# Experts' results written over their gathered rows, without clearings, finished in groups of four

## The chip, the core and the metric

The kernel runs on one core of a Trainium2 chip. A core has five engines with queues of their own that work in order: TensorE (PE, its weight loads listed as PEld), VectorE (DVE), ScalarE (ACT), GpSimd (POOL) and SyncE (SP). They wait for each other by semaphores, and transfers run beside them. The metric is the device time of one execution in microseconds (us), the median of several runs.

## What is computed

A batch of 4 sequences of 1024 tokens of 256 numbers passes two layers, each with a residual: causal attention of 16 heads, and then a block with a second, small attention over the 4 sequences and a mixture of 8 experts. Only the experts' end matters here:

```python
h = _layernorm(x + attn_out, ln1_g, ln1_b)
flat = h.reshape(-1, C)
...
_, top_i = jax.lax.top_k(probs, 2)
assign = jnp.max(top_i, axis=-1)
...
for e in range(E):
    he = jax.nn.gelu(flat @ w1[e].T + b1[e], approximate=False)
    oe = he @ w2[e].T + b2[e]
    out = jnp.where((assign == e)[:, None], oe, out)
moe_out = out.reshape(T, B, C)
return _layernorm(h + moe_out, ln2_g, ln2_b)
```

Each token has one expert. Its row `h` goes through that expert, `h` is added, the sum is normalised, scaled by `ln2_g`, and the shift `ln2_b` and the residual are added.

## The kernel before

Most of the program is attention, and a scheduler written in Python lays out every engine's instructions by hand while the program is built. The change touches only the last stage, the tiles of the experts. Tokens are sorted by expert into 38 tiles of 128 rows. A first lot of 18 tiles (named 0_0 to 0_17) can be listed when six of the eight blocks of tokens are routed; the second lot of 20 (1_0 to 1_19) is listed after the last block (`tabulate_rest`, at about 745 us). A tile lives in a row buffer `given` of 128 x 512 numbers: the left half is `h`, the right half the residual plus `ln2_b`. There are 18 such buffers, used in turn, so tile 1_j takes the one of 0_j, and 1_18 and 1_19 those of 1_0 and 1_1.

Work on the tiles goes in steps (`tile_step`). A step calls `fetch`, which gathers one tile by an indirect DMA on POOL (L1813), then `finish` and then the stages A, B and C of three tiles, which I name so: A turns the rows (`mtp`, copied to `mt` by ScalarE), B is the hidden product (`hid`) and its Gelu (`ge`), C is the output product (`oe`). Two tiles' `oe` share one PSUM bank; in the second lot these are 1_1 with 1_2, 1_3 with 1_4 and so on. In most tiles of the second lot `h` is added on VectorE, in place over the left half of `given`; in the first lot and in the last two tiles PE adds it in PSUM (`by_product`).

Counting steps from the start, tile 1_j is gathered in step 23+j, has A in step 28+j, B in 29+j and C in 30+j. `finish` first takes each pair that is being finished one stage further, and then takes the next two tiles that are done. The stages of a pair of the second lot, tiles k and k+1 with k even, are:

- step 32+k: the adds, the statistics (`stats_v`, `mv_v`), `rstd` + eps on VectorE, and the root, a power of -1/2, on POOL (`norm_root`, L814);
- step 33+k: nothing, while tiles are waiting;
- step 34+k: on VectorE two operations per tile, (v - mean) x gain into a tile `o` (a ring of four buffers), and `o` x `rstd` + right half of `given`;
- step 35+k: for each tile on POOL a clearing of an unused tile (`spare`, L1928) and a scatter of `o` to the output, an indirect DMA (L1929).

When no tile is waiting any more (`experts.waiting()` is 0) the later stages run together: in step 48 the pair 14/15 has its results and its scatters, and 16/17 its root; 1_18 and 1_19 are finished singly, in steps 49 to 51. After step 32 VectorE also checks the softmax sums (`check_sums`), and after step 35 PE and VectorE form `odd`, which decides at the end whether a slower general program has to run.

Of the kernel before, what the change touches and what calls it, by code (L numbers as in the profile page):

```python
# [29 lines left out]
F32 = mybir.dt.float32  # L30
# [3 lines left out]
ALU = mybir.AluOpType  # L34
# [3 lines left out]
P = 128  # L38
B, T, C = 4, 1024, 256
# [46 lines left out]
B_IN, B_OUT, G1, B1, G2, B2, RB = 0, 3 * C, 4 * C, 5 * C, 6 * C, 7 * C, 8 * C  # L86
# [519 lines left out]
def fast_layer(ctx: ExitStack, tc: tile.TileContext, odd, x, wq, wk, wv, wp, w_in, w_out, w_r,  # L606
# [26 lines left out]
    nc = Core(tc.nc, told)  # L633
# [14 lines left out]
    def const(name, shape, dtype=F32, into=keep):  # L648
        return into.tile(shape, dtype, tag=name, name=name)
# [73 lines left out]
    def row(at, n=C):  # L723
        return row_sb[:, at - G1:at - G1 + n]
# [66 lines left out]
    def norm_tiles(name, tag=""):  # L791
        return [
            small.tile([P, B] + shape, F32, tag=kind + tag, name=f"{kind}_{name}")
            for kind, shape in (("stats", [6]), ("mv", [2]), ("rstd", []))
        ]

    def norm_one(tiles, i, src):
        stats, mv, _ = tiles
        nc.vector.bn_stats(stats[:, i], src)
        nc.vector.bn_aggr(mv[:, i], stats[:, i])  # L800

    def norm_end(tiles, n):
        _, mv, rstd = tiles
        nc.vector.tensor_scalar(rstd[:, :n], mv[:, :n, 1], EPS, None, ALU.add)
        return mv, rstd

    def norm_stats(src, n, name, tag=""):
        tiles = norm_tiles(name, tag)
        for i in range(n):
            norm_one(tiles, i, src(i))  # L810
        return norm_end(tiles, n)

    def norm_root(rstd, n):
        nc.gpsimd.tensor_tensor(  # L814
            rstd[:, :n], rstd[:, :n], minus_half.to_broadcast([P, n]), ALU.pow
        )
# [344 lines left out]
    class Routing:  # L1161
# [3 lines left out]
        def __init__(self):  # L1165
            self.placed = 0
# [270 lines left out]
    class Table:  # L1437
        pass

    spare = const("spare", [P, 1])  # L1440
    part = Routing()
    tables = []
    tiles_to_do = []
# [357 lines left out]
    late = {}  # L1801
# [97 lines left out]
                nc.tensor.matmul(self.v, ident, self.hx[:, :C], start=False, stop=False)  # L1899
            nc.tensor.matmul(self.v, sel, b_bf[1], start=False, stop=True)  # L1900

    def finish_tiles(two):

        n, name = len(two), two[0].name
        for t in two:
            if not t.by_product:
                own = t.hx[:, :C]
                nc.vector.tensor_tensor(own, own, t.v, ALU.add)
                t.v = own
        mv, rstd = norm_stats(lambda k: two[k].v, n, f"v_{name}", "_v")  # L1910
        norm_root(rstd, n)
        yield
        if experts.waiting():
            yield
        os = []
        for k, t in enumerate(two):
            o = late["work"].tile([P, C], F32, tag="o", name=f"o_{t.name}", bufs=4)
            nc.vector.scalar_tensor_tensor(
                o, t.v, mv[:, k, 0:1], row(G2), ALU.subtract, ALU.mult
            )  # L1920
            nc.vector.scalar_tensor_tensor(
                o, o, rstd[:, k:k + 1], t.hx[:, C:2 * C], ALU.mult, ALU.add
            )
            os.append(o)
        if experts.waiting():
            yield
        for t, o in zip(two, os):
            nc.gpsimd.memset(spare, 0.0)  # L1928
            ins = nc.gpsimd.indirect_dma_start(  # L1929
                out=out.rearrange("t n c -> (t n) c"),  # L1930
                out_offset=bass.IndirectOffsetOnAxis(ap=t.table.out_rows[:, t.j:t.j + 1], axis=0),
                in_=o, in_offset=None, bounds_check=B * T - 1, oob_is_err=False,
            )
            if late["n_out"]:
                tc.declare_no_dep(ins.ins, group="rows", reason="a token is in one tile")
            tc.add_to_no_dep_group("rows", ins.ins)
            late["n_out"] += 1

    class Experts:
# [3 lines left out]
        def __init__(self):  # L1943
            self.step, self.fetched = 0, []
            self.n_fetched = self.n_finished = 0
            self.under_way, self.done, self.finishing = [], [], []

        def fetch(self):
            self.step += 1
# [9 lines left out]
        def finish(self):  # L1959
            for it in list(self.finishing):  # L1960
                n, stages = it
                if next(stages, self) is self:
                    self.finishing.remove(it)
                    self.n_finished += n
            n = 1 if self.done and len(self.done) + len(self.under_way) + self.waiting() < 3 else 2
            if len(self.done) >= n:
                two, self.done = self.done[:n], self.done[n:]
                self.finishing.append((len(two), finish_tiles(two)))
                next(self.finishing[-1][1])

        def waiting(self):
            return len(tiles_to_do) + len(self.fetched)

        def left(self):
            return (len(tiles_to_do) + len(self.fetched)
                    + len(self.under_way) + len(self.done) + len(self.finishing))

        def advance(self, finish=True):
            if finish:
# [18 lines left out]
    experts = Experts()  # L1998


    class Running:
# [4 lines left out]
        def next(self):  # L2006
            self.kind = next(self.stages, "end")
            if self.kind != "end":
                self.kind, self.cost, *self.more = self.kind
# [261 lines left out]
    work = ctx.enter_context(pool("work", 2))  # L2271
# [76 lines left out]
    def tile_step(finish=True):  # L2348
        at = tile_begin()
        for on, cost in TILE:  # L2350
            if on != "DVE" or experts.finishing or len(experts.done) == 2:
                free[on] = max(free[on], at) + cost
        experts.fetch()
        experts.advance(finish)
# [21 lines left out]
    n = 0  # L2376
# [11 lines left out]
@with_exitstack  # L2388
def tile_layer(ctx: ExitStack, tc: tile.TileContext, *args):
    nc = tc.nc  # L2390
    flag = ctx.enter_context(tc.tile_pool(name="flag", bufs=1))
    odd = flag.tile([P, 1], I32, tag="odd", name="odd")
    fast_layer(tc, odd, *args)
    again = nc.values_load(
        odd[0:1, 0:1], min_val=0, max_val=1,
        skip_runtime_bounds_check_because="a comparison's result",
    )
    with tc.If(again > 0):
        general_layer(tc, *args)
# [75 lines left out]
```

## Time and profile before

| | us |
|---|---|
| median of 3 runs (836.48 to 842.09) | 839.2 |
| the profiled run | 839.28 |
| its span, from the first to the last instruction | 837.1 |
| last gather starts | 805.38 |
| last stage C on PE ends | 821.44 |
| last scatter starts | 828.95 |

The mean granted TensorE clock of the profiled run is 0.94. Busy over the span are PE 719.4 us (86%), DVE 544.6 (65%), ACT 416.6 (50%) and POOL 251.1 (30%). In tenths of each of 40 slices of the span (some 21 us each) POOL and PE read so:

```profile
PE   4988879995999999998989999999983689678982
...
POOL 5534102211113221102211212122130235637885
```

POOL works little in the middle of the program and most in the last five slices, which are the stage that the change touches. A timeline line reads: start, duration, engine, source line, operation, out<-in, count, and in brackets the idle time of the engine just before it with what ended that idle time. All instructions that pass through the wrapper of line 587 carry that line's number, so groups are told apart by their tiles.

### The profile page before, as it was taken

How to read it: one execution, taken by the hardware profiler on the slowest of the kernel's cores; microseconds unless marked ns; L12 is line 12 of the kernel's file. 1: busy time of each engine (PE TensorE's matmuls, PEld its weight loads, DVE VectorE, ACT ScalarE, POOL GpSimd, SP SyncE). 2: the span in 40 equal slices, each digit the busy share in tenths (PEclk: the TensorE clock that was granted, in tenths of full speed). 3: DMA queues.
4: the chain of work that ended last, by engine and by line, in shares of the span. 5: the costliest groups of instructions: out<-in, count | busy, mean ns of one | idle time of the engine just before them, and what ended most of it. 6: DMA issues, size and time to landing. Idle time of an engine off the chain costs nothing. (4 is left out here: it accounts for less than half of the span.)

```text
span 837.1 us, 22503 instructions
## 1 busy us (share of the span) xinstructions
PE 719.4 (86%) x8917; PEld 540.2 (65%) x8917; DVE 544.6 (65%) x1316; ACT 416.6 (50%) x625; POOL 251.1 (30%) x360
## 2 busy tenths in 40 slices
PE   4988879995999999998989999999983689678982
PEld 2766657674666756665667767787762368567772
DVE  7337224546678877946964739487695869884663
ACT  1455436563647556735654658578460235323540
POOL 5534102211113221102211212122130235637885
PEclk9799889998999999998999999999997699978997
DMA  7454444424344324333354635445315512333430
GB/s 215 117 148 137 143 134 134 144 63 123 94 119 129 108 77 147 98 104 95 93 142 141 185 109 144 123 126 158 94 53 195 177 37 90 93 97 120 124 103 24
DMA packets 75219, 99.56 MB, mean 119 GB/s; under 512 B 19496, under 2 KB 58723, under 8 KB 74596
## 3 DMA queue, kind: packets, MB, share of 16 engines
q1 hardware_dynamic: 64576, 79.63, 32.1%
q0 software_dynamic: 4864, 14.16, 5.6%
q10 hardware_dynamic: 5668, 4.25, 1.7%
q8 instruction: 73, 1.20, 0.6%
q14 instruction: 38, 0.31, 0.1%
HBM read 61.55 MB, written 35.12 MB: 115 GB/s over the span
## 5 line engine op out<-in xcount | busy, mean ns | idle before, releaser
L587 ACT ACTIVATE p<-sk 128x1024 f32<-128x1024 f32 (+1 forms) x320 | 287.0, 939 | 162.8 <-PE sk L587 147.8
L986 POOL TENSOR_SCALAR_AFFINE_SELECT p<-p 128x512 f32<-128x512 f32 (+1 forms) x160 | 103.6, 651 | 397.8 <-ACT p L587 395.9
L587 PE MATMUL sk<-slots 32*128 32x128 f32 (+1 forms) x3456 | 181.7, 328 | 21.2 <-DVE kq L587 10.0
L587 PEld LDWEIGHTS sk<-slots 32*128 32x128 f32 x3456 | 138.1, 188 | 64.9 <-issue 26.8
L587 PE MATMUL pv<-p,v 128*32 128x128 f32 (+1 forms) x3456 | 144.5, 314 | 10.4 <-ACT p L587 4.6
L587 PEld LDWEIGHTS pv<-p,v 128*32 128x32 f32 x3456 | 96.7, 111 | 48.3 <-issue 8.3
L587 PE MATMUL qkvp<-w_in,ut 128*128 128x264 f32 (+1 forms) x224 | 79.1, 489 | 0.0
L587 PEld LDWEIGHTS qkvp<-w_in,ut 128*128 128x128 f32 x224 | 40.3, 194 | 26.7 <-issue 22.4
L587 PE MATMUL oe<-w,ge 128*128 (+1 forms) x152 | 45.2, 423 | 12.9 <-DVE given L587 4.5
L587 PE MATMUL qkp<-xt,wqk 128*128 128x256 f32 x208 | 54.4, 407 | 0.2 <-ACT p L587 0.2
L1813 POOL DMA_INDIRECT given<-rows,rows x38 | 43.2, 1137 | 27.6 <-DVE at_t L587 11.6
L587 PE MATMUL hid<-mt,w 128*128 128x128 f32 x304 | 47.0, 293 | 0.5 <-ACT ge L587 0.5
L587 PEld LDWEIGHTS qkp<-xt,wqk 128*128 128x128 f32 x208 | 39.6, 200 | 11.1 <-issue 3.3
L587 ACT COPY qkv<-qkvp 128x512 f32<-128x512 f32 (+1 forms) x28 | 15.3, 555 | 58.5 <-PE qkvp L587 43.9
L587 PEld LDWEIGHTS hid<-mt,w 128*128 128x128 f32 x304 | 41.9, 200 | 2.0 <-ACT ge L587 1.0
L587 DVE COPY qkv<-qkvp 128x264 f32<-128x264 f32 x28 | 11.9, 431 | 46.9 <-PE qkvp L587 46.8
L1929 POOL DMA_INDIRECT out_dram<-o,out_rows x38 | 38.9, 1024 | 8.8 <-issue 6.3
L587 DVE TENSOR_REDUCE sc<-pr 128x64 f32<-128x1024 f32 x32 | 39.0, 1220 | 1.1
L587 PEld LDWEIGHTS oe<-w,ge 128*128 128x128 f32 x152 | 28.0, 205 | 17.8 <-DVE given L587 5.7
L587 DVE TENSOR_TENSOR pv<-qkv,sc 128x1024 f32<-128x1024 f32 x32 | 39.2, 1224 | 0.4 <-issue 0.3
L587 DVE TENSOR_TENSOR pr<-qkv 128x1024 f32<-128x1024 f32 x32 | 39.2, 1226 | 0.0
L587 PE MATMUL vp<-wv,xt 128*128 128x256 f32 x128 | 35.3, 423 | 0.0
(333 smaller groups left out, 1040.2 us busy)
## 6 DMA issues: line engine op xcount, KB each, us to landing
slots<-k SPq DMA_DIRECT2D x128, 80.0 KB
k<-kq SPq DMA_DIRECT2D x32, 256.0 KB
v<-v SPq DMA_DIRECT2D x16, 288.0 KB
v<-v SPq DMA_DIRECT2D x4, 1152.0 KB
x<-in_x_dram SPq DMA_DIRECT2D x16, 256.0 KB
y<-yt SPq DMA_DIRECT2D x16, 256.0 KB
rows<-x SPq DMA_DIRECT2D x32, 128.0 KB
slots<-k SPq DMA_DIRECT2D x64, 64.0 KB
```

The lines of the kernel that those rows point to most:

```text
L587: ins = made(*args, **kwargs)
L986: nc.gpsimd.affine_select(blocks, blocks, pattern=[[0, 2], [0, size], [1, P]], compare_op=ALU.is_ge, fill=0.0, base=0, channel_multiplier=-1,)
L1813: nc.gpsimd.indirect_dma_start(out=self.hx, out_offset=None, in_=t.rows_of, in_offset=bass.IndirectOffsetOnAxis(ap=t.rows_[:, self.j:self. ...
L1929: ins = nc.gpsimd.indirect_dma_start(out=out.rearrange("t n c -> (t n) c"), out_offset=bass.IndirectOffsetOnAxis(ap=t.table.out_rows[:, t. ...
```

## The change

Results go over the left half of `given`, where the rows `h` were, instead of into a tile `o`. The clearing before each scatter is gone. Taking a pair is split into `measure_tiles` (adds and statistics) and `finish_tiles` (root, results, scatters), and a group of tiles is finished when it holds tiles added by PE, or four tiles, or when fewer than four tiles are still on their way. The first lot and tiles 1_18 and 1_19 stay in the groups they had. In a group of four the results and the scatters are given out two tiles per step while tiles are waiting.

```diff
-    spare = const("spare", [P, 1])
...
-    def finish_tiles(two):
+    def measure_tiles(tiles, two):
+        if not tiles:
+            tiles.extend([norm_tiles(f"v_{two[0].name}", "_v"), []])
+        norms, group = tiles
         for t in two:
             if not t.by_product:
                 own = t.hx[:, :C]
                 nc.vector.tensor_tensor(own, own, t.v, ALU.add)
                 t.v = own
-        mv, rstd = norm_stats(lambda k: two[k].v, n, f"v_{name}", "_v")
+        for t in two:
+            norm_one(norms, len(group), t.v)
+            group.append(t)
+
+    def finish_tiles(norms, group):
+        n = len(group)
+        mv, rstd = norm_end(norms, n)
         norm_root(rstd, n)
         yield
         if experts.waiting():
             yield
-        os = []
-        for k, t in enumerate(two):
-            o = late["work"].tile([P, C], F32, tag="o", name=f"o_{t.name}", bufs=4)
...
+        for lo in range(0, n, 2):
+            if lo and experts.waiting():
+                yield
+            for k, t in list(enumerate(group))[lo:lo + 2]:
+                o = t.hx[:, :C]
...
         if experts.waiting():
             yield
-        for t, o in zip(two, os):
-            nc.gpsimd.memset(spare, 0.0)
+        for k, t in enumerate(group):
+            if k == 2 and experts.waiting():
+                yield
+            o = t.hx[:, :C]
             ins = nc.gpsimd.indirect_dma_start(
...
-                self.finishing.append((len(two), finish_tiles(two)))
-                next(self.finishing[-1][1])
+                measure_tiles(self.measured, two)
+                in_psum = any(t.by_product for t in self.measured[1])
+                if in_psum or len(self.measured[1]) > 2 or self.open() < 4:
+                    norms, group = self.measured
+                    self.measured = []
+                    self.finishing.append((len(group), finish_tiles(norms, group)))
+                    next(self.finishing[-1][1])
+
+        def open(self):
+            return self.waiting() + len(self.under_way) + len(self.done)
```

A row buffer is counted as free for the next gather when the finishing of its whole group has been issued, as before.

## The prediction

> **What bounds the kernel now.** I read the page's chain of waits first. It ends on the GpSimd queue and stays there almost without a break from 744 us on, so what the last 85 us cost is read from POOL, not from PE with its 86% of the span.
>
> ```profile
> POOL 6%; issue 3%; DVE 1%; PE 1%; POOLq 0%
> ```
>
> Then the busy time by stretch (us of the stretch, then PE, PEld, DVE, ACT, POOL busy, granted clock, DMA share, GB/s):
>
> ```profile
> 744.60:770.00 25.40, 18.54 (x99) 15.68 (x98) 13.90 (x44) 6.97 (x16) 19.99 (x28) 0.80 0.41 125
> 770.00:807.40 37.40, 32.75 (x236) 28.56 (x235) 24.24 (x72) 18.93 (x42) 31.90 (x44) 1.00 0.39 118
> 807.40:821.20 13.80, 12.38 (x85) 10.77 (x84) 10.64 (x33) 4.27 (x10) 10.97 (x17) 1.00 0.24 79
> ```
>
> POOL's 31.9 of 37.4 us looks like spare time, but the timeline of POOL alone shows that there is none. This is one pair of tiles of the second lot:
>
> ```profile
> 788.74 1.27 POOL L1813 DMA_INDIRECT given<-rows,rows  x1 [0.19 <-PE hid L587]
> 790.01 0.11 POOL L1928 MEMSET spare<- 128x1 f32 x1
> 790.31 1.03 POOL L1929 DMA_INDIRECT out_dram<-o,out_rows  x1 [0.19 <-issue]
> 791.34 0.12 POOL L1928 MEMSET spare<- 128x1 f32 x1
> 791.64 1.00 POOL L1929 DMA_INDIRECT out_dram<-o,out_rows  x1 [0.19 <-issue]
> 792.95 1.06 POOL L1813 DMA_INDIRECT given<-rows,rows  x1 [0.30 <-issue]
> 794.02 0.74 POOL L814 TENSOR_TENSOR rstd_v<-rstd_v,minus_half 128x2 f32<-128x2 f32 x1
> 794.96 1.27 POOL L1813 DMA_INDIRECT given<-rows,rows  x1 [0.20 <-issue]
> ```
>
> Only the short gaps between instructions are free. The pair takes 6.22 us (788.74 to 794.96); PE needs 2.31 us per tile where it does not wait (stage C at 770.56 to 772.86), 4.62 per pair. POOL is the bound there. Who passes its lateness on, from the waits of 745 to 830 us (total, times, longest):
>
> ```profile
> DVE o L587 <- DMA out_dram<-o,out_rows: 10.1, 5, 4.7
> DVE o L587 <- POOL rstd_v L814: 10.0, 10, 2.3
> ...
> PE oe L587 <- DVE given L587: 4.5, 4, 1.4
> ...
> PE oe L587 <- DVE stats_v L587: 4.2, 1, 4.2
> ```
>
> VectorE stands at a pair's second operation until the root comes, or before its first until an old `o` buffer has been written out; the next pair's adds stand behind it, and stage C on PE behind the adds.
>
> **What the Trainium skill says.** "Perfetto Trace Analysis", GPSIMD Engine Instruction: a GpSimd span is unreliable, time it by start-to-start spacing; I do. The same page, DMA Instruction — SWDGE (GPSIMD): the recorded end is the last descriptor written, not the data landed. The trace agrees: a scatter records 1.0 us, but VectorE waited for the one of 755.23 until 758.61, 3.4 us after its start (748.56 to 751.92 gives 3.4 too). "DMA: Bandwidth & Descriptors", Two DMAs through the same engine are not ordered: a gather over a row that a scatter still reads must wait for that scatter's semaphore. No wait of that kind exists before; the change makes one. "PSUM — Partial Sum Buffer", PSUM bank collisions: two engines' accesses to one bank have to be kept apart. The trace agrees: stage C of 1_12 (803.13) began when the add of 1_11, in the other half of its bank, was over.
>
> **Clearings.** 38 leave, 32 of them after 744. A gather after a gather takes 1.31 without one (744.62 to 745.93), a scatter to the next gather 1.30 (756.55 to 757.85), a scatter to the next scatter with one 1.32 or 1.33. So the clearing lies in the gap that is there anyway, and I take 0.01 each, nothing in the sum. Bounds: 0.31 saved (all between recorded end 791.34 and next start 791.64), if the stamps hide it; or 0.05 lost, the scatter of the spacings above, if a scatter straight behind another is dearer. With some 25 scatters on the path: -7.8 to +1.3 us.
>
> **Results over the rows.** The operations stay 0.48 us each. The wait for `o` buffers goes. It cost most in the first lot's end: VectorE stood 4.71 us before 758.61, so stage C of 0_16 waited 4.17 (to 761.51), and POOL then idled 0.44 before the root of 761.97 and 1.59 before that of 769.51. Now VectorE, free at 753.9, ends 0_12 and 0_13 near 755.9 and the statistics of 0_15 near 756.8; stage C of 0_16 starts at 757.4. Roots 14/15 and 16/17 find their input ready, 765.3 against POOL's slot at 767.5: POOL gains 0.44 + 1.59 = 2.0. The new wait: gather 1_18 needs scatter 1_0 landed. That is 785.6 + 3.4 = 789.0 in the sum below, and the gather comes at 794.6: nothing. For the gathers of 1_2 to 1_17 the distance is four steps or more. If it did wait, the other gather and the scatters behind it on POOL would shift by the same.
>
> **Groups of four.** Of the nine pair roots of the second lot eight become four roots of four, and one (16/17) stays. A root and its gap take 0.93 (794.02 to 794.96, 787.81 to 788.74); a root of four is seen in another stage:
>
> ```profile
> L814 POOL TENSOR_TENSOR rstd_h<-rstd_h,minus_half x8: 1006/1024/1947, 250.4 to 726.2; 128x4 f32<-128x4 f32 x8
> ```
>
> 1.02 + 0.2 = 1.22, so four tiles save 2 x 0.93 - 1.22 = 0.64 (bounds: 0.93 if a root of four cost what one of two does, -0.3 with the longest of the row, 1.95), four groups 2.6 us of POOL (3.7 to -1.2). That the groups do not form is excluded by the code: with 20 tiles coming, four or more are open at every pair but the last. The four `rstd` additions on VectorE (0.17) that go are off the path. More important, the order moves. Root g (tiles 4g to 4g+3) is issued in step 34+4g, the first two results in 36+4g, the other two in 37+4g, scatters in 38+4g and 39+4g; before, scatters came three steps after each pair's root. So gathers 12 to 15 no longer have scatters between them, and the scatters are pushed to the end. SP issues nothing from 745 us on, so it is moved past by nothing.
>
> **The sum, along POOL** (1.31 per DMA, 1.46 for one behind a root). Gather 9 is at 772.6 (774.62 - 2.0); root 0/1 is gone, so gather 10 at 773.9; scatters 0_16, 0_17 at 775.2, 776.5; gather 11 at 777.9; root 0 at 779.0, its statistics ready near 776 (adds 2/3 once stage C of 1_3 is done at 774, after the check of sums' 2.1 us). Gathers 12 to 15: 780.2, 781.7, 783.0, 784.3. Scatters 0, 1: 785.6, 786.9. Root 1 at 788.0 (statistics ready 787.6). Gather 16 at 789.2; scatters 2, 3: 790.7, 792.0; gathers 17 to 19: 793.3, 794.6, 795.9 (before 805.38); scatters 4, 5: 797.2, 798.5; root 2 from 799.6 to 800.6. Until here POOL is the bound. Then VectorE: results 8, 9 to 802.1, adds 12/13 to 802.9, which lets stage C of 1_14 begin, at 803 (before 809.37). Stage C of 1_15 ends at 806.4; adds, two statistics and `rstd` end at 808.2; root 3 from 808.3 to 809.3 (before, the root of 14/15 was at 815.03). POOL waits a little before it. Now the bill: behind root 3 stand scatters 10 to 15, six and not four, before root 16/17, because step 48 has no tile waiting and puts four in one go: 809.5, 811.0, 812.3, 813.6, 814.9, 816.2, root at 817.3 to 817.6 (stamps of 0.3 spread). It was at 821.21: 3.7 us earlier. From there the chain (two scatters, root, scatter, root, scatter, landing) is as before, since 1_18 and 1_19 still end singly: 837.1 - 3.7 = 833.4. The profiled run took 839.28 with a span of 837.1, 2.2 more, and the median of the runs is 839.2: 835.6.
>
> **The rivals.** *Clearing was dear* (0.12): each held POOL 0.31; 7.8 us more go, 828. For it: GpSimd stamps are rough. Against it: DMA spacings with and without are equal.
> *The bill wins, slower* (0.15): the pile at the end is one mechanism, two more scatters and a longer root ahead of root 16/17, 2 x 1.31 + 0.3 = 2.9 to 3.1 us. It decides if the statistics of 14/15 come less than 3.1 us earlier than 814.94. That is so if PE or VectorE, not POOL, set the pace in 770 to 807: then 842.3 at worst. For it: PE at 0.66 clock in 760 to 770, where ten us of its work could not be hastened. Against it: PE waits 1.3 to 1.4 us per pair for adds.
> *The same time* (0.13): the 2.0 us of the first lot's end do not come, since root 16/17 then waits for PE as now; 1.7 us remain, 837.5, within the runs' own spread of 836.5 to 842.1.
> *My sum* (0.60): 835.6, with its own range 833 to 838.5.
>
> **How the numbers follow.** 1% is 8.4 us, about what a measurement can tell from no change. Only the dear clearing passes it, and not always: faster 0.12 (with a little for a run that is low anyway). The bill alone reaches +3, so slower is 0.03, the rest is the same. For 8 in 10 the range goes from 830.5, which takes in a part of the dear clearing, to 841, which takes in most of the bill.
>
> **What would show it.** Right: no `o` wait on `out_dram`; roots of 128x4 near 1.02; the last gather near 796; stage C of 1_14 near 803; six scatters in a row near 810 to 817. Wrong: scatter spacing not 1.3, a gather that waits for a scatter, roots of four above 1.3, a last root of four later than 812.

## The result, and the profile after

The changed kernel takes 840.84 us (median of 20 runs, 835.26 to 847.54), the kernel before 836.43 us beside it (20 runs): a ratio of 1.0046, 95% interval 1.0027 to 1.0064. It is slower by 4.4 us in the medians, where 3.7 us less were forecast. The profiled run took 840.12 us, its span is 838.4 us.

The chain of waits of the kernel after no longer lies on POOL (6% of the span before, 1% now). The chain of before reaches back only to the start of this stage and that of after through the whole program, so the other shares can't be compared:

```profile
PE 56%; DVE 26%; DMA 7%; issue 5%; SPq 2%; ACT 2%; POOL 1%; ACTq 0%; POOLq 0%; DVEq 0%
```

The busy time by stretch, in the stretches shown of before:

```profile
744.60:770.00 25.40, 19.23 (x125) 16.55 (x124) 14.70 (x44) 9.62 (x21) 20.86 (x21) 0.93 0.42 126
770.00:807.40 37.40, 31.51 (x200) 27.00 (x200) 21.49 (x65) 15.10 (x34) 28.70 (x28) 0.91 0.43 126
807.40:821.20 13.80, 12.45 (x87) 10.95 (x85) 10.34 (x31) 4.42 (x11) 6.64 (x7) 1.00 0.13 44
```

From 770 to 807 POOL is busy for 28.7 us and not 31.9, as intended. But PE is less busy too (31.5 against 32.8), and at a granted clock of 0.91 where before had 1.00. At 770 it was ahead of before, with 125 instructions against 99; by 807 it is behind, with 325 against 335. The relief of POOL did not reach PE. The timeline of POOL shows where its saved time went:

```profile
789.42 1.14 POOL L814 TENSOR_TENSOR rstd_v<-rstd_v,minus_half 128x4 f32<-128x4 f32 x1 [1.67 <-DVE rstd_v L587]
...
801.26 1.07 POOL L814 TENSOR_TENSOR rstd_v<-rstd_v,minus_half 128x4 f32<-128x4 f32 x1
...
813.36 1.14 POOL L814 TENSOR_TENSOR rstd_v<-rstd_v,minus_half 128x4 f32<-128x4 f32 x1 [5.74 <-DVE rstd_v L587]
814.70 1.22 POOL L1942 DMA_INDIRECT out_dram<-given,out_rows  x1 [0.20 <-issue]
816.23 0.99 POOL L1942 DMA_INDIRECT out_dram<-given,out_rows  x1 [0.31 <-issue]
817.52 1.10 POOL L1942 DMA_INDIRECT out_dram<-given,out_rows  x1 [0.30 <-issue]
818.92 0.98 POOL L1942 DMA_INDIRECT out_dram<-given,out_rows  x1 [0.30 <-issue]
820.21 0.98 POOL L1942 DMA_INDIRECT out_dram<-given,out_rows  x1 [0.30 <-issue]
821.50 0.98 POOL L1942 DMA_INDIRECT out_dram<-given,out_rows  x1 [0.30 <-issue]
822.50 0.74 POOL L814 TENSOR_TENSOR rstd_v<-rstd_v,minus_half 128x2 f32<-128x2 f32 x1
```

POOL stands for 1.67 us before root 1 and for 5.74 us before root 3, waiting for statistics of tiles; then six scatters stand before the root of 16/17. These two idle times, 7.4 us, are the waits of POOL for `rstd` in the list of waits of 745 to 832 us.

Why are the statistics late? This is the timeline of all engines around tile 1_13, whose `hid` ends with the first two lines:

```profile
797.69 0.66 PE L587 MATMUL hid<-mt,w 128*128 128x128 f32 x4
798.19 0.22 PE L587 MATMUL hid<-chosen,b_bf 128*128 128x128 bf16 x1
798.51 1.13 PE L587 MATMUL oe<-w,ge 128*128 x4
...
802.41 0.38 ACT L587 ACTIVATE ge<-hid 128x256 f32<-128x256 f32 x1 [3.26 <-remote]
802.85 1.05 PE L587 MATMUL hid<-mt,w 128*128 128x128 f32 x4 [2.88 <-issue]
...
804.87 1.88 PE L587 MATMUL oe<-w,ge 128*128 x4
...
806.90 0.42 DVE L587 TENSOR_TENSOR given<-given,oe 128x256 f32<-128x256 f32 x1 [2.80 <-PE oe L587]
```

`hid` is over at 798.41 by the record (798.19 + 0.22), yet the Gelu, which in the program waits only for it and for older work of ScalarE, starts at 802.41. 0.1 us lies between them where nothing is wrong, 0.65 at most in this stage of the profile of before where ScalarE was free (793.22 to 793.87). The next `hid` waits for that Gelu, so PE stands for 2.88 us, and then runs at half the clock: `oe` takes 1.88 us and not 1.13. The add, the statistics and root 3 come behind. A first such place lies at 776.91, where `hid` of 1_6 is over and its Gelu starts at 779.53:

```profile
776.69 0.22 PE L587 MATMUL hid<-chosen,b_bf 128*128 128x128 bf16 x1
...
777.77 0.17 PE L587 MATMUL n_badp<-n_bad,ones_bf 128*128 128x1 bf16 x1
...
779.53 0.38 ACT L587 ACTIVATE ge<-hid 128x256 f32<-128x256 f32 x1 [2.54 <-PE mtp L587]
779.55 0.16 DVE L587 TENSOR_SCALAR odd<-n_badp 128x1 int32<-128x1 f32 x1 [4.47 <-PE mtp L587]
...
779.97 0.71 PE L587 MATMUL hid<-mt,w 128*128 128x128 f32 x4 [1.75 <-ACT ge L587]
...
782.32 1.85 PE L587 MATMUL oe<-w,ge 128*128 x4 [1.03 <-DVE given L587]
```

Not only ScalarE is late here: VectorE's `odd` waits for `n_badp`, which is over at 777.94 by the record, and starts 0.02 us after the Gelu. Two engines that wait for TensorE go on together, so what is late is TensorE's completions. PE stands for 1.75 us and then for 1.03 us, and again runs at half the clock. The Trainium skill, "Perfetto Trace Analysis", Tensor Engine Instruction, says that a matmul's recorded end is computed and that its semaphore is pushed when PSUM has acknowledged the bytes; so the waiters, and not the record, tell when it was over. The same skill, "TensorE: Matmul & The Clock Gate", What's actually happening, puts the half clock behind an idle window of about 3.4 us; here one recorded gap of 2.9 us was enough, and single gaps of 1.5 us in the kernel before were not.

One thing that could hold engines up without showing among their waits are the transfers that fetch instructions; the page lists them as queues of their own kind. At the second place, at 802, it is not they: from 792 to 813 us the trace has one queue alone at work, that of the gathers and scatters (packets, MB, share of the 16 engines):

```profile
q0 software_dynamic: 704, 1.93, 32.1%
```

### The profile page after: what moved, and what is told of

Its sections match the earlier page's. It is cut to its first block, busy times and chain, and to the rows that moved or that the text cites. A ratio compares the mean times of both kernels' runs of the same rounds, so it can differ in the third digit from the quotient of the medians.

```text
span 838.4 us, 22477 instructions
## 1 busy us (share of the span) xinstructions
PE 719.0 (86%) x8917; PEld 540.3 (64%) x8917; DVE 542.9 (65%) x1312; ACT 416.8 (50%) x625; POOL 249.3 (30%) x318
## 3 DMA queue, kind: packets, MB, share of 16 engines
q1 hardware_dynamic: 64576, 79.63, 31.9%
## 4 chain that ended last, share of the span: by engine, by line
PE 56%; DVE 26%; DMA 7%; issue 5%; SPq 2%; ACT 2%; POOL 1%; ACTq 0%; POOLq 0%; DVEq 0%
PE sk L587 13%; PE pv L587 11%; PE qkvp L587 8%; PE qkp L587 6%; PE vp L587 5%; DVE pv L587 4%; PE ao L587 3%; PE oe L587 3%; DVE given L587 2%; DVE sc L587 2%; DVE u L587 2%; PE op L587 2%; DVE pr L587 2%; ACT p L587 2%; PE hid L587 2%
## 5 line engine op out<-in xcount | busy, mean ns | idle before, releaser
L986 POOL TENSOR_SCALAR_AFFINE_SELECT p<-p 128x512 f32<-128x512 f32 (+1 forms) x160 | 106.7, 671 | 395.4 <-ACT p L587 393.5
L1942 POOL DMA_INDIRECT out_dram<-given,out_rows x38 | 39.0, 1027 | 12.9 <-issue 8.0
L587 DVE COPY qkv<-qkvp 128x264 f32<-128x264 f32 x28 | 11.9, 431 | 46.1 <-PE qkvp L587 46.0
```

The costliest lines, as they stand in the source:

```text
L587: ins = made(*args, **kwargs)
L986: nc.gpsimd.affine_select(blocks, blocks, pattern=[[0, 2], [0, size], [1, P]], compare_op=ALU.is_ge, fill=0.0, base=0, channel_multiplier=-1,)
L1942: ins = nc.gpsimd.indirect_dma_start(out=out.rearrange("t n c -> (t n) c"), out_offset=bass.IndirectOffsetOnAxis(ap=t.table.out_rows[:, t. ...
```

## The experiments

A ratio is always to the kernel before, run beside it. The runs were made in five series, in which the median of the kernel before lay between 836.16 and 837.25 us; where runs of different series are compared below, the text says so. "Stage" is the time from the first gather of the second lot to the end of the profiled span. It helps to compare single profiles, since that gather started anywhere from 740.1 to 746.7 us although all kernels do the same up to it.

| run | median, us | ratio, 95% interval | stage, us |
|---|---|---|---|
| before (profile shown above) | | 1 | 92.5 |
| after, again | 844.01 | 1.0075, 1.0043 to 1.0107 | 98.0 |
| pairs | 835.22 | 0.9977, 0.9960 to 0.9995 | 91.4 |
| before, no clearings | 837.24 | 0.9993, 0.9972 to 1.0014 | 92.3 |
| two groups, then pairs | 840.16 | 1.0035, 1.0014 to 1.0057 | 97.1 |
| pairs, then two groups | 837.88 | 1.0005, 0.9984 to 1.0027 | 95.1 |
| pairs, no roots | 843.17 | 1.0075, 1.0044 to 1.0105 | 100.0 |
| groups, no roots | 843.03 | 1.0064, 1.0035 to 1.0093 | 97.4 |
| pairs, every other unused root | 841.30 | 1.0054, 1.0030 to 1.0077 | 98.0 |
| pairs, unused roots | 836.31 | 0.9988, 0.9963 to 1.0013 | 92.2 |
| pairs, double roots | 842.50 | 1.0051, 1.0026 to 1.0075 | 94.9 |
| groups with pauses | 837.34 | 1.0011, 0.9991 to 1.0030 | 92.6 |
| groups, pause at the root | 845.71 | 1.0104, 1.0058 to 1.0149 | 99.8 |
| two groups with pauses, then pairs | 835.80 | 0.9994, 0.9975 to 1.0012 | 91.6 |
| groups, half gathers | 839.48 | 1.0036, 1.0016 to 1.0055 | 93.6 |
| groups, gathers of nothing | 847.00 | 1.0108, 1.0078 to 1.0138 | 103.0 |
| groups, fixed w2 | 839.03 | 1.0043, 1.0019 to 1.0068 | 93.4 |
| groups, fixed w1 | 839.77 | 1.0024, 1.0005 to 1.0042 | 97.1 |
| pairs, fixed w2 | 834.88 | 0.9982, 0.9967 to 0.9997 | 91.3 |


I went in with three theories. **A**, the bill: six scatters and not four stand behind the last group of four, and root 3 is not early enough to pay for them. **B**, the stalls: TensorE's late completions and the half clock behind them, brought about by the new order. **C**: the missing clearings or the results over the rows cost something.

### Which part of the change costs

The changed kernel again, without an edit:

> The changed kernel as it is, profiled a second time. Theory A (the bill): the time is 1.0046 of the kernel before again, and the last 30 us look the same: six scatters behind the root of tiles 12 to 15, the root of 16/17 some 2.5 us later than before when counted from the first gather of the second lot. Whether PE stood still twice on the way is chance: the two stalls of 2.9 us before hid of tile 1_7 (779.97) and of 1_14 (802.85) are gone or elsewhere. Theory B (the stalls): the time is 1.0046 again and the two stalls come again at the same two tiles, each about 2.9 us long and followed by some 3 us at half the granted clock, since the order of the gathers makes them.

Its second stall is at the same tile as in the first profile (`hid` of 1_14, 2.54 us). The first, which was 1.75 us in that profile and not the 2.9 us that I wrote above, is split over neighbouring tiles:

```profile
775.04 0.71 PE L587 MATMUL hid<-mt,w 128*128 128x128 f32 x4 [1.76 <-issue]
777.90 1.69 PE L587 MATMUL oe<-w,ge 128*128 x4 [1.54 <-issue]
...
805.04 0.71 PE L587 MATMUL hid<-mt,w 128*128 128x128 f32 x4 [2.54 <-issue]
806.71 2.02 PE L587 MATMUL oe<-w,ge 128*128 x4
```

The stalls come in both profiles of the kernel. From the root of 12 to 15 to the end it takes 25.0 us in both profiles of the changed kernel (838.4 - 813.36), against 22.1 from the root of 14/15 before (837.1 - 815.03). The bill of the two more scatters is there, 3.0 us, as well as the stalls.

Pairs:

```diff
-                if in_psum or len(self.measured[1]) > 2 or self.open() < 4:
+                if in_psum or len(self.measured[1]) > 1 or self.open() < 4:
```

> The changed kernel, but each pair is finished by itself as in the kernel before (results over the rows and no clearings stay, the groups go). Theory A: no pile of six, so what is left is the gain of the rows, the 2 us that the wait for the result buffers cost at the first lot's end: 834.4 us beside 836.4 of the kernel before, a ratio of 0.9975. Theory B: the same, because four gathers no longer follow each other and the stalls go with them. Theory C (the missing clearings or the results over the rows are what costs): as slow as the changed kernel, a ratio of 1.0046.

Faster than before, by 1.9 us (0.0023 of 837.25), and 8.8 us faster than the changed kernel beside it. Theory C falls: the groups cost everything. This version beats both kernels, the one before by 0.2%.

The kernel before without clearings:

```diff
-            nc.gpsimd.memset(spare, 0.0)
```

> The kernel before with the clearings at the scatters left out and nothing else. Theories A and B: no difference, 836.4 us, within 0.4 us, and scatters that follow each other stay 1.31 to 1.33 us apart. Theory C: up to 4 us slower, a ratio of 1.0046, with scatters further apart or transfers that take longer.

No difference that can be told, as expected.

Groups first, and groups last (`self.open()` falls from 18 at the first pair to 10 at tiles 8/9):

```diff
-                if in_psum or len(self.measured[1]) > 2 or self.open() < 4:
+                if in_psum or len(self.measured[1]) > 2 or self.open() < 12:
```

> The changed kernel with groups of four for tiles 0 to 7 of the second lot and pairs from tile 8 on: the tail is that of the kernel before, the grouping earlier stays. Theory A: the pile of six before the root of 16/17 is gone (four scatters there), so this gets what the prediction promised for two groups, 834 us, a ratio of 0.997. Theory B: the first stall (before hid of 1_7) comes with the first groups and stays, the second goes: half of the loss, about 838 us, a ratio of 1.002.

```diff
-                if in_psum or len(self.measured[1]) > 2 or self.open() < 4:
+                if in_psum or len(self.measured[1]) > 2 or not 4 <= self.open() < 12:
```

> The complement of the run with two groups first: pairs for tiles 0 to 7 of the second lot, groups of four for 8 to 15. Theory A: the pile of six stays, so this is 3 us slower than pairs throughout, 838.3 us, a ratio of 1.0015, and the root of 16/17 has six scatters ahead of it. Theory B: the loss is spread over the groups by their number: two groups of four cost about half of what four cost, 4 us above pairs; the stall before hid of 1_14, which came in both profiles of the changed kernel, comes again.

The first two groups alone lose 4.9 us against pairs, without any bill at the end: theory A doesn't suffice. The last two alone lose 2.7 us (in another series), about the bill, though PE stood there too, one tile later than expected (1.94 us before the `mtp` at 805.21). Together 7.6 of the 8.8 us.

### Is POOL the bound?

The roots of tiles 0 to 15 left out, in pairs and in groups:

```diff
-        norm_root(rstd, n)
+        if group[0].by_product or group[0].j >= 16:
+            norm_root(rstd, n)
```

> The kernel finished in pairs (results over the rows, no clearings), with the eight roots of tiles 0 to 15 of the second lot left out, so its output is not normalised there. It takes 8 x 0.93 = 7.4 us of GpSimd time away and changes no order. Theory P (GpSimd is the bound of the stage from 770 to 807, as the prediction had it): 5 to 7 us below the pairs with their roots, 829 us, a ratio of about 0.99. Theory B (TensorE with its late completions is as close to being the bound): no more than 2 us below, 833.5 us, a ratio of 0.995, and GpSimd idles the rest.

> The changed kernel with the four roots of its groups of four left out, so its output is not normalised there. Theory R (the groups lose because VectorE stands at a group's results until the one late root comes, with the adds behind it): as fast as the pairs without roots or nearly, 5 us or more below the changed kernel. Theory A (the pile of six scatters behind the last group): at most 2 us below the changed kernel, since the last four tiles' statistics still come when TensorE allows and six scatters still stand behind them. Theory B: the late completions of TensorE stay, the gain is 1 to 3 us.

Both expectations fail, and not by size: with 7.4 us of work less on POOL and no root to wait for, the pairs become 8.0 us slower (843.17 against 835.22 in another series; the intervals of the ratios are far apart). In groups nothing is gained, so theory R, the one late root, falls as well. PE in the pairs without roots:

```profile
783.70 0.86 PE L587 MATMUL hid<-mt,w 128*128 128x128 f32 x4 [3.17 <-issue]
787.37 2.07 PE L587 MATMUL oe<-w,ge 128*128 x4 [1.64 <-DVE given L587]
...
802.29 1.22 PE L587 MATMUL hid<-mt,w 128*128 128x128 f32 x4 [2.41 <-ACT ge L587]
804.48 2.02 PE L587 MATMUL oe<-w,ge 128*128 x4
```

The same picture as in the changed kernel, worse: stalls of 3.17 and 2.41 us, and matmuls of 2.0 us behind them. What the two have in common is a GpSimd queue with indirect DMAs for long stretches and no compute instruction between them. That is theory S.

In the pairs without roots, the same roots on a tile of ones (`ones2`, 128 x 2) that nobody waits for, all eight, and every other one (these lines follow those of the edit above):

```diff
+        else:
+            nc.gpsimd.tensor_tensor(ones2, ones2, minus_half.to_broadcast([P, 2]), ALU.pow)
```

> The pairs without roots (843.2 us, 8 us above the pairs with roots), but where each of the eight roots stood GpSimd takes the same root of a tile of ones that nobody waits for; the output is not normalised for tiles 0 to 15 of the second lot. VectorE still waits for no root. Theory S (a stream of indirect DMAs without a pause makes TensorE's completions late, and the roots were the pauses): back to the pairs with roots, 835 us, a ratio of 0.998. Theory W (what costs is that VectorE no longer waits, so TensorE runs ahead into a wait): as slow as without roots, a ratio of 1.0075.

```diff
+        elif group[0].j % 4 == 0:
+            nc.gpsimd.tensor_tensor(ones2, ones2, minus_half.to_broadcast([P, 2]), ALU.pow)
```

> The pairs without waiting for roots, with every other unused root (tiles 0, 4, 8, 12): runs twice as long as with all eight, and half the pauses. Theory S: in between, 839.5 us, a ratio of 1.003. If any pause is enough: as with all eight, 0.999.

Useless work brings the time back: 0.9988 with eight pauses, 1.0054 with four, 1.0075 with none. VectorE waits for no root in any of the three, so theory W falls. Over the 38 us that begin 25 us after the first gather, the busy times are these, first with eight:

```profile
770.80:808.80 38.00, 31.20 (x197) 25.59 (x197) 24.00 (x71) 15.11 (x35) 30.91 (x32) 0.95 0.40 127
```

with four:

```profile
766.00:804.00 38.00, 28.01 (x155) 23.32 (x155) 19.11 (x56) 12.25 (x27) 27.09 (x27) 0.77 0.41 121
```

and with none:

```profile
766.40:804.40 38.00, 24.10 (x141) 19.63 (x140) 20.35 (x61) 10.89 (x24) 24.61 (x24) 0.87 0.40 124
```

PE gets through 197, 155 and 141 matmuls in the same time, and its clock is lower in the last two. POOL gets through 32, 27 and 24 instructions, but 6, 3 and 0 of them are the unused roots: it issues 26, 24 and 24 DMAs. So with less to do it issues no more of them, and waits instead; without roots it waits 3.2 us of this stretch for VectorE's results, with eight unused roots 0.6.

In the pairs with their own roots, twice the root, the second unused:

```diff
         norm_root(rstd, n)
+        if not group[0].by_product and group[0].j < 16:
+            nc.gpsimd.tensor_tensor(ones2, ones2, minus_half.to_broadcast([P, 2]), ALU.pow)
```

> The pairs with their roots, and behind each of the eight roots of tiles 0 to 15 a second one of ones that nobody waits for: 8 x 0.75 = 6 us more on GpSimd. Theory P (GpSimd is the bound of 770 to 807): 5 to 6 us above the pairs, 840.5 us, a ratio of 1.004. Theory S: the longer pauses give back as late completions what they cost, within 2 us of the pairs.

7.3 us above the pairs (in another series; 6.2 by the ratios), so theory P holds here: with pauses as long as these, POOL is the bound and its added time, some 6 us, counts in full. Of the amounts tried, that of the pairs is the best, and nobody chose it.

### Pauses in the groups

An unused root at the pair that does not end a group, and the same four straight behind the groups' own roots (the edit of the double roots, in the groups):

```diff
                     next(self.finishing[-1][1])
+                else:
+                    nc.gpsimd.tensor_tensor(ones2, ones2, minus_half.to_broadcast([P, 2]), ALU.pow)
```

> The changed kernel, and at the pair of each group that does not end it (tiles 0/1, 4/5, 8/9, 12/13) GpSimd takes a root of a 128 x 2 tile of ones that nobody waits for: 4 x 0.93 = 3.7 us more work on the engine that the prediction called the bound. Theory S: faster than the changed kernel by 2 to 5 us, since the run of DMAs is broken again. Theory P (GpSimd's time counts): slower by up to 3.7 us. If the groups' late results are the cause, no change within 1 us.

> The changed kernel with the same four unused roots as the groups with pauses, but each straight behind its group's own root, so that the runs of indirect DMAs between the roots stay as long as in the changed kernel (six and eight). Theory S (long runs are what hurts): no help, as slow as the changed kernel or up to 3 us slower, a ratio of 1.005 to 1.010. If it is only that GpSimd's pace is lower: as the groups with pauses, a ratio of 1.001.

With 3.7 us more work in the runs of DMAs the groups come down to 1.0011; with the same work where it breaks no run they go up to 1.0104. The intervals don't touch. The place of a pause decides, not the amount of work.

The bill by itself: the groups with pauses, but pairs from tile 8 on.

```diff
-                if in_psum or len(self.measured[1]) > 2 or self.open() < 4:
+                if in_psum or len(self.measured[1]) > 2 or self.open() < 12:
```

> Groups of four with the unused root between for tiles 0 to 7, pairs from tile 8 on. Theory S with the bill: the stalls stay away and only four scatters stand before the root of 16/17, so this is 2.5 to 3 us below the groups with pauses throughout: 834.5 us, a ratio of 0.9975, and from the root of 14/15 to the end 22 us, not 25. Theory S without a bill: as the groups with pauses, a ratio of 1.001.

The tail is as expected. In the groups with pauses the last root of four and the root of 16/17 are

```profile
812.23 1.20 POOL L814 TENSOR_TENSOR rstd_v<-rstd_v,minus_half 128x4 f32<-128x4 f32 x1 [1.54 <-DVE rstd_v L587]
...
821.42 0.73 POOL L814 TENSOR_TENSOR rstd_v<-rstd_v,minus_half 128x2 f32<-128x2 f32 x1
```

and with pairs from tile 8 on

```profile
810.63 0.82 POOL L814 TENSOR_TENSOR rstd_v<-rstd_v,minus_half 128x2 f32<-128x2 f32 x1 [0.81 <-DVE rstd_v L587]
...
816.75 0.73 POOL L814 TENSOR_TENSOR rstd_v<-rstd_v,minus_half 128x2 f32<-128x2 f32 x1
```

9.2 us from root to root against 6.1, and 25.1 to the end against 22.1. In the medians only 1.5 us of it are seen (835.8 against 837.3, in different series, and the intervals overlap), so of the 3.0 us some was given back elsewhere.

### What makes TensorE's completions late

Half the bytes of each gather, and gathers of next to nothing:

```diff
+            if t.n == 1 and not self.by_product:
+                n, rows_of = C, t.rows_of.rearrange("n (h c) -> (n h) c", h=2)
```

> The changed kernel, but each gather of tiles 0 to 17 of the second lot brings one half of a row's bytes (128 x 256 and not 128 x 512), so those tiles compute on other data; the instructions and their order stay. If TensorE's late completions come from the transfers of gathers that follow each other closely, they go, and the time falls by 4 us or more, to a ratio below 1.0. If the transfers have nothing to do with it, the time stays within 1 us of the changed kernel, a ratio of 1.0046 to 1.0075, and the completions are as late as before.

```diff
-                bounds_check=t.n_rows - 1, oob_is_err=False,
+                bounds_check=t.n_rows - 1 if t.n == 0 or self.by_product else 0, oob_is_err=False,
```

> The changed kernel, but the gathers of tiles 0 to 17 of the second lot are told that every row but the first is out of bounds, so they move next to nothing and those tiles compute on older data; GpSimd issues the same instructions in the same order. If the late completions come from the bytes on their way, they go: 5 us or more below the changed kernel. If they come from GpSimd's issuing of indirect DMAs one behind the other, they stay, and the time is within 1 us of the changed kernel.

Half the bytes change little (1.0036, inside the interval of the changed kernel's first series). Without bytes it is the slowest of all, which neither expectation had and which stays unexplained. The window of that kernel shows the DMA share halved, 0.20 where the others have 0.40, and PE no better off:

```profile
771.70:809.70 38.00, 30.54 (x190) 25.71 (x190) 19.88 (x60) 15.04 (x33) 23.91 (x24) 0.90 0.20 58
```

A Gelu starts as late as 792.04 for a `hid` that is over at 787.83. The bytes of the gathers are not the cause. Those of the scatters were left as they were.

The register loads of TensorE (in stage B, for w2) and of ScalarE (in the copy of w1); the same edit in each place, and TensorE's in the pairs too:

```diff
-                at = nc.values_load(
+                at = 0 if self.table.n == 1 else nc.values_load(
```

> The changed kernel, but TensorE takes the second weight of every tile of the second lot from one fixed expert: it loads no offset into a register there, and the output is computed with other weights. If TensorE's late completions come from its register loads being held up while GpSimd issues DMAs, they go, and with them the half clock behind them: 5 us or more below the changed kernel, a ratio of 0.999 or less. If not, the time stays at a ratio of 1.0046 to 1.0075 and completions stay 2 to 4 us late in places.

> The pairs with their roots and TensorE's second weight from one fixed expert. If TensorE's register loads are the cause of late completions, but the pairs hide these behind GpSimd's pace, this gains no more than 1 us over the pairs (a ratio of 0.997), while the same edit in the groups gains 5. If the register loads cost everywhere alike, it gains as much as in the groups.

> The same for ScalarE: the first weight of every tile of the second lot is copied from one fixed expert, with no register load on ScalarE. If ScalarE's register loads hold it up so that it sees TensorE late, the gain is 5 us or more; otherwise none, a ratio of 1.0046 to 1.0075.

Fixed w2 gives 1.0043 in the groups and 0.9982 in the pairs, fixed w1 1.0024 (1.0005 to 1.0042, median 839.77): TensorE's loads are not the cause, and at most a small part may be ScalarE's. Without them a Gelu still starts at 803.86 for a `hid` that is over at 800.57.

What stays open is how a run of indirect DMAs slows PE, and whether it is by holding TensorE's completions back. That pauses are the remedy, by their place and their number, is shown; that they work by letting completions through is not. Late Gelus come in fast kernels too. ScalarE stood for one 1.9 us in the pairs and 2.5 us in the kernel before without clearings:

```profile
762.48 0.38 ACT L587 ACTIVATE ge<-hid 128x256 f32<-128x256 f32 x1 [1.91 <-PE mtp L587]
```

```profile
786.58 0.38 ACT L587 ACTIVATE ge<-hid 128x256 f32<-128x256 f32 x1 [2.46 <-remote]
```

With all eight unused roots Gelus are up to 2.6 us late, but PE lost less by them than without roots (31.2 us busy against 24.1). The longest such stands, 3.3 to 4.8 us, are in slow kernels, with one profile of each: the changed one, the pairs without roots and those with every other unused root. It may be that pauses keep PE from the long waits behind which its clock is halved. Keeping the run of DMAs and slowing PE by itself was not tried.

## Why the prediction was wrong

**Clearings at nothing: right.** 0.9993, and 1.32 us from scatter to scatter without one (785.42 to 786.74).

**Results over the rows, 2.0 us: right in its cause, and near in size by the medians alone.** The pairs, which have only this and the missing clearings, gain 1.9 us (0.4 to 3.3 by the interval). No wait for `out_dram` is left, and no gather waits for a scatter. But at the place that the sum named the gain is smaller: gather 9 should have come 28.0 us after the first gather of the lot. It came at 28.7 in the pairs and 29.0 in the changed kernel, against 30.0 before, and the stage of the pairs is 1.1 us shorter.

**Roots of four near 1.02: right enough.** 1.05 to 1.14.

**The bill of 2.9 to 3.1 us: right.** 3.0 in two profiles.

**"Until here POOL is the bound. Then VectorE: ... which lets stage C of 1_14 begin, at 803": this step failed.** Its ground was that PE, which needs 2.31 us per tile where it does not wait, would follow at that pace once POOL let it. Counted from the first gather, root 1 should have come at 43.4 us and came at 46.1, root 2 at 55.0 and came at 57.9, so PE was late, and POOL stood 1.67 us for it before root 1, where the sum still took POOL for the bound; stage C of 1_14 should have come at 58.4 and came at 64.6 (807.97 - 743.33); root 3 should have come at 63.7 and came at 70.0. So root 3 was 0.4 us earlier than the root of 14/15 before (70.4) and not the 6.7 of the sum; 0.4 against a bill of 3.0 is 2.6 us more, which is the difference of the stages (95.1 against 92.5). In the profile PE, let go, stood for 1.75 and then 1.03 us around 780 and for 2.88 us at 802, both times because completions of its own matmuls came late, and both times went on at half the clock (`oe` 1.85 and 1.88 us). The roots that the groups took away for 0.64 us per four tiles were worth more as breaks than as time saved. Why completions come late is open.

**The rivals.** "The bill wins, slower" came true, at the point that it named: the statistics of the last pair came less than 3.1 us earlier. What I held against it, that PE waits 1.3 to 1.4 us per pair for adds, I read as room that PE could use. It was no room that PE used: with the waits gone, longer ones came. That the time, 840.84, lies inside the range, at its upper edge of 841, is luck: the range was laid around a kernel before of 839.2 us, which took 836.43 in 20 runs, and 4.4 us more than 839.2 would have been 843.6. And that less work on POOL could cost time I had in no case.

## What to carry to other kernels

The pace of an engine that is held back by another is not known from its time per tile where it runs freely; before counting on it, take the brake away in one run and look (here: leave the roots out). Where an engine issues indirect DMAs and short compute instructions in turn, the compute instructions between them may be worth keeping, and a regrouping that makes the runs of DMAs longer is to be tested apart from the work that it saves. And count what stands behind the last batch: groups of four put two more scatters, 3 us, on the end.

## What was not expected of the hardware

- About 7.4 us of GpSimd work (8 roots at 0.93) taken away made the kernel 8.0 us slower, and the same work put back for nobody made it as fast again within the noise (0.9977, 1.0075, 0.9988).
- In the stage where GpSimd issues indirect DMAs, TensorE's completions can reach their waiters up to 4 us after the recorded end, with or without bytes behind the gathers (802.41 for 798.41; 792.04 for 787.83 without bytes), and two waiting engines see them at the same time (779.53 and 779.55).
- One recorded gap of 2.5 to 3.2 us on TensorE was followed by half the clock, and so were two of 1.8 and 1.5 us close together; single gaps of 1.5 us in the kernel before were not. In between the recorded gap does not decide: one of 1.94 us before 805.21 was followed by an `oe` of 1.85 us in "pairs, then two groups", and several of the same length in the double roots were not, with an `oe` of 1.13 us:

```profile
793.17 1.13 PE L587 MATMUL oe<-w,ge 128*128 x4 [1.95 <-DVE given L587]
```
